# A wait in every third indirect transfer of a four-layer kernel, and a new order table

## The chip, the cores and the metric

The program runs on 1 core of one Trainium2 chip. The metric is device time in microseconds, from launch to the end of the program. The time of a kernel is the median over its runs; for the kernel before, six runs gave 665.21 to 668.11 us, median 667.08. Beside the timed runs there is one profiled execution, whose trace the views below come from.

The core has five engines that each run their own list of instructions in order: PE (matmuls; its weight loads are listed as PEld), DVE and ACT (vector and scalar work), POOL (slower vector work, and here all indirect transfers) and SP (it only issues transfers). They meet through semaphores. 16 DMA engines move the data.

## The reference, cut to what matters

The input is `x` of shape 8 x 512 x 128, that is 4096 tokens of 128 features. Four layers follow each other, each added to its input:

```python
x = x + L0_attn(layernorm(x))   # gated linear recurrence over 512 steps, 128 channels
x = x + L0_ffn(layernorm(x))    # one 128x128 linear, chosen among 8 by logits and noise
x = x + L1_attn(layernorm(x))   # delta rule: 16 heads, an 8x8 state each, 512 steps
x = x + L1_ffn(layernorm(x))    # mixture of experts
```

The last layer is the one that the change is about. For each token it picks two of eight experts:

```python
probs = softmax(xf @ w_router)
topk_w, topk_idx = top_k(probs, 2)
h = gelu(einsum('te,ieh->tih', xf, w1) + b1)      # 128 -> 512
out = einsum('tih,ihe->tie', h, w2) + b2          # 512 -> 128
out = sum(out * weights[..., None], axis=1)       # two experts have a weight
```

and the third layer fixes the pace of much of the kernel, since its state goes from step to step:

```python
retrieval = einsum('bhij,bhj->bhi', S, k_t)
S = S + einsum('bhi,bhj->bhij', beta_t * (v_t - retrieval), k_t)
o_t = einsum('bhij,bhj->bhi', S, q_t)
```

## The kernel before

**Tiles and groups.** A tile is 16 time steps of all 8 sequences, 128 rows. There are 32 tiles, taken in nine groups of 2, 4, 4, 4, 4, 4, 4, 4 and 2 (`SIZES`). Each group goes through the first two layers, then through the delta rule, whose steps are taken four at a time: 4 blocks a tile, 128 blocks in all, each a fixed row of DVE instructions (`prod`, `st`, `so`). The groups overlap: while DVE works on the blocks of one, ACT, PE and POOL prepare the next ones (`f`, `knq`, `dots`, `tmat`) and finish the earlier ones (`so`, `qkp`).

**The experts.** After the delta rule `route` finds each token's two experts. Groups are put together to sets (`GROUPS`: 2; 4+4; 4+4; 4+4; 4 tiles), five sets in all; the last group of 2 tiles is computed with every expert instead. For a set, `experts` computes on DVE a place for each row, sorted by expert and padded to whole blocks of 128 rows (`dest`, shown as `small_dest`). Then:

1. `scatter` sends each tile's rows to their places in a table in DRAM: one indirect transfer of 128 rows of 512 bytes for each tile and each of the two choices, issued by POOL (`places<-xne,small_dest`). That makes 4, 16, 16, 16 and 8 transfers, 60 in all.
2. `load_rows` reads four blocks of the sorted rows back (`xb<-places`, issued by SP). It waits for all scatters of the set.
3. PE transposes them (`ph<-ident,xb`), ACT copies the result (`xbT`), and for each block SP loads the weights of its expert (`w1b`), PE multiplies (`ph<-xbT,w1b`), ACT applies the gelu (`hid`), PE multiplies again (`po<-w_sb,hid`, or `in<-w_sb,hid` where another bank is used), and SP writes the outcome to a second table (`results<-yb`).
4. 60 indirect transfers fetch each token's two rows (`back<-results,small_dest`, POOL). They are weighted on ACT and summed on POOL (`fin`), for the last set both on DVE, and go out through DRAM (`out_rows`, `out`).

Two more indirect transfers fetch the weights of the second layer (`wsel`, `bsel`), so there are 122.

**The order.** No engine's order follows from the order of the source. All operations are first recorded in a `Plan` (`Recorder.record`, hence one line, L330, for most instructions) with their dependencies. A planner (`place`, `backward`) can put them in an order by costs and due times; there an indirect transfer starts no earlier than `WINDOW` microseconds after the one `BURST` places before it (`rows[-BURST] + WINDOW`), 6.0 us and 4 places. When the table `ORDER` has as many entries as there are operations, the planner is not used: `emit` goes through the 4796 numbers of `ORDER`, and `BANKS` gives the PSUM bank of each tile that has a choice. Each engine then executes its own operations in that order. POOL's operations are each tied to the one before; between scatters of one set some of these ties are dropped together with the dependency between their rows, so that scatters of one set can change places among themselves.

An indirect transfer occupies POOL while it is issued, and lands later. Its landing is told by one of eight semaphores, taken in turn, so a transfer waits, before and after the change, for the one eight before it.

**Names used below.** A "set" is one of the five groups of rows that go through the experts together. "The fourth set" has the 16 scatters between 473.5 and 503.5 us, "the fifth set" the 8 scatters between 545.6 and 556.8 us.

Of the kernel before, what the change touches and what calls it, by code (L numbers as in the profile page):

```python
# [69 lines left out]
class Plan:  # L70
# [4 lines left out]
    def __init__(self, tc, banks):  # L75
        self.tc, self.hw, self.banks = tc, tc.nc, banks
        self.ops, self.seen, self.key, self.slack = [], {}, 0.0, 0.0
        self.tensor, self.vector, self.scalar, self.gpsimd, self.sync = (
            Recorder(self, e) for e in ("tensor", "vector", "scalar", "gpsimd", "sync")
        )  # L80
# [213 lines left out]
    def emit(self):  # L294
        kind = mybir.EngineType
        with self.tc.manual_schedule(engines={kind.PE, kind.DVE, kind.Activation, kind.SP}):
            for op, switch in self.best():
                if switch:
                    self.hw.scalar.preload_act_table_set(switch)  # L299
                made = op.emit()  # L300
                if op.engine == "gpsimd":
                    self.tc.keep_in_program_order(made)

# [50 lines left out]
def _cost(engine, name, n, kw):  # L354
# [19 lines left out]
BURST, WINDOW = 4, 6.0  # L374
# [9 lines left out]
    3, 10, 38, 43, 36, 37, 45, 35, 34, 48, 44, 1, 5, 53, 0, 9, 50, 49, 57, 46, 7, 335, 52, 8, 11, 32, 51, 47, 33, 4,  # L384
    12, 59, 126, 39, 61, 58, 31, 2, 13, 6, 16, 14, 327, 67, 62, 15, 40, 129, 63, 17, 64, 54, 130, 65, 18, 131, 336,
    66, 19, 343, 132, 21, 323, 133, 435, 55, 134, 324, 830, 135, 68, 153, 70, 145, 154, 328, 69, 146, 106, 444, 160,
    101, 107, 100, 325, 77, 152, 42, 147, 163, 60, 108, 326, 102, 155, 161, 390, 103, 391, 104, 392, 337, 148, 393,
    109, 344, 338, 156, 110, 112, 71, 149, 394, 87, 111, 41, 150, 98, 136, 157, 113, 151, 339, 367, 399, 158, 114,
    162, 340, 418, 137, 351, 159, 72, 165, 164, 400, 329, 375, 167, 341, 401, 330, 56, 397, 359, 405, 115, 74, 166,
    128, 395, 331, 116, 168, 406, 117, 22, 342, 332, 118, 176, 105, 170, 407, 119, 398, 169, 29, 171, 182, 175, 185,  # L390
    120, 333, 172, 138, 183, 173, 73, 174, 184, 334, 396, 187, 408, 402, 423, 188, 177, 409, 191, 139, 178, 403, 80,
    197, 179, 180, 181, 140, 99, 186, 141, 205, 346, 142, 192, 189, 410, 193, 404, 190, 345, 198, 199, 411, 194, 81,
    195, 200, 196, 204, 347, 206, 207, 201, 202, 209, 422, 203, 143, 412, 208, 210, 211, 348, 413, 213, 212, 214,
    219, 414, 446, 220, 215, 221, 226, 445, 222, 216, 349, 90, 415, 23, 223, 217, 224, 416, 218, 225, 417, 227, 447,
    229, 420, 228, 91, 231, 448, 419, 449, 424, 450, 230, 232, 144, 233, 421, 425, 236, 451, 235, 360, 237, 452, 241,
    427, 383, 238, 453, 249, 239, 234, 352, 240, 121, 243, 368, 250, 428, 458, 27, 20, 350, 253, 242, 460, 244, 254,
    429, 248, 258, 257, 245, 246, 251, 459, 247, 259, 263, 252, 271, 464, 260, 255, 261, 262, 272, 465, 256, 275,
    265, 454, 466, 276, 280, 281, 264, 455, 307, 426, 266, 282, 122, 279, 283, 270, 267, 284, 273, 268, 285, 269,
    293, 481, 274, 309, 277, 294, 297, 278, 286, 287, 298, 288, 301, 456, 292, 467, 289, 290, 291, 295, 362, 302,
    457, 361, 303, 468, 296, 461, 299, 88, 354, 300, 462, 353, 304, 384, 89, 469, 305, 25, 363, 313, 306, 355, 312,  # L400
    92, 376, 315, 463, 316, 24, 317, 318, 319, 320, 93, 470, 321, 364, 356, 430, 84, 322, 641, 431, 127, 432, 78,
    433, 28, 85, 434, 314, 365, 436, 30, 477, 437, 311, 471, 310, 308, 438, 79, 439, 440, 385, 94, 472, 123, 473, 95,
    124, 644, 82, 96, 125, 643, 645, 474, 441, 83, 442, 642, 475, 443, 499, 86, 482, 357, 358, 515, 517, 487, 516,
    518, 476, 519, 369, 522, 386, 521, 479, 523, 1065, 524, 478, 483, 520, 646, 525, 647, 484, 648, 649, 480, 783,
    650, 740, 377, 526, 378, 485, 527, 370, 486, 528, 379, 371, 655, 677, 488, 657, 489, 372, 490, 380, 373, 491,
    492, 656, 494, 651, 493, 387, 661, 388, 389, 653, 495, 662, 496, 652, 663, 366, 497, 664, 529, 97, 654, 26, 665,
    509, 659, 498, 658, 530, 666, 531, 660, 532, 500, 667, 501, 533, 502, 504, 534, 505, 503, 506, 535, 507, 1066,
    536, 508, 668, 381, 537, 548, 374, 547, 510, 538, 545, 511, 1068, 512, 546, 549, 669, 539, 513, 550, 540, 514,
    543, 695, 551, 541, 711, 552, 575, 1069, 576, 573, 670, 544, 578, 577, 554, 712, 574, 542, 714, 579, 553, 580,
    555, 558, 678, 671, 586, 581, 560, 382, 559, 557, 562, 672, 561, 563, 556, 582, 564, 673, 565, 592, 566, 583,  # L410
    567, 675, 568, 584, 569, 593, 585, 715, 594, 713, 595, 588, 674, 679, 596, 716, 590, 717, 597, 676, 589, 718,
    754, 680, 599, 587, 600, 719, 755, 682, 598, 720, 605, 601, 721, 681, 722, 591, 723, 602, 683, 724, 606, 725,
    603, 570, 614, 726, 1067, 684, 604, 571, 727, 685, 572, 728, 686, 729, 1070, 687, 619, 613, 730, 1071, 1413, 688,
    1072, 731, 1073, 607, 689, 617, 1074, 732, 690, 611, 733, 608, 734, 753, 735, 618, 691, 609, 615, 736, 692, 738,
    737, 610, 620, 739, 625, 757, 1136, 741, 616, 693, 758, 621, 694, 759, 696, 760, 622, 626, 697, 761, 612, 742,
    627, 699, 743, 1137, 762, 1079, 698, 629, 1135, 756, 623, 763, 624, 744, 628, 764, 1081, 745, 765, 1075, 766,
    1080, 630, 767, 1085, 746, 768, 1077, 631, 1086, 769, 1076, 1087, 747, 770, 771, 748, 772, 749, 632, 773, 1088,
    774, 700, 633, 701, 1078, 775, 702, 634, 703, 750, 1089, 776, 705, 777, 635, 778, 779, 636, 780, 781, 637, 1416,
    1138, 1090, 784, 1178, 1082, 751, 1139, 785, 752, 1140, 786, 1179, 1141, 1415, 1083, 787, 704, 1142, 1177, 1164,
    788, 1414, 1143, 706, 1417, 789, 707, 1084, 1144, 790, 708, 1145, 709, 1146, 1418, 1091, 1147, 791, 710, 1419,  # L420
    1148, 1102, 1149, 1150, 1420, 782, 999, 1092, 1151, 1000, 1152, 1119, 792, 1153, 1093, 793, 1154, 794, 1155,
    1421, 1094, 795, 1002, 1422, 1206, 1156, 1157, 638, 1101, 796, 1158, 797, 1001, 1159, 1095, 1160, 1162, 1003,
    1161, 1096, 1004, 1005, 1097, 1010, 1180, 1165, 1220, 1166, 1181, 1099, 1221, 639, 1182, 1167, 1014, 1183, 1168,
    1007, 1184, 1219, 1098, 1169, 640, 1006, 1185, 1008, 1016, 1103, 1170, 1009, 1163, 1017, 1171, 1186, 1018, 1019,
    1187, 1172, 1100, 1104, 1020, 1173, 1174, 1012, 1021, 1013, 1188, 1105, 1189, 1106, 1107, 1190, 1022, 1191, 1023,
    1175, 2111, 1192, 1176, 1024, 1193, 1194, 1195, 1108, 1025, 1196, 1197, 1026, 1029, 1198, 1027, 1109, 1199, 1030,
    1028, 1200, 1110, 1201, 1111, 1031, 1202, 1112, 1043, 1037, 1203, 1204, 1427, 1032, 1222, 1262, 1113, 1205, 1038,
    1035, 1223, 1429, 1224, 1114, 1041, 1033, 1225, 1248, 1207, 1226, 1115, 1261, 798, 1428, 1208, 1040, 1227, 1209,
    1034, 1039, 1042, 1228, 1210, 1011, 1211, 1116, 1229, 1433, 1015, 1230, 1044, 1036, 1231, 799, 1232, 1263, 1434,
    1212, 1117, 1233, 1046, 1264, 1045, 1435, 1234, 1049, 1425, 1235, 1047, 1050, 1236, 1048, 1237, 1213, 1423, 1426,  # L430
    1238, 1052, 1239, 1214, 1051, 1240, 1215, 1053, 1241, 1216, 1424, 1242, 1217, 1243, 75, 1129, 1118, 1244, 1054,
    1246, 1218, 1436, 1245, 1247, 1304, 1437, 1249, 1482, 1265, 1250, 1055, 1266, 1251, 1267, 1431, 1268, 1252, 1253,
    1269, 1120, 1481, 1123, 1254, 1270, 1430, 1121, 1255, 76, 1483, 1271, 1256, 1122, 1124, 800, 1257, 1272, 1056,
    1273, 1438, 802, 1274, 1125, 1258, 1432, 1126, 1275, 1259, 1127, 1276, 1260, 1439, 801, 1595, 1277, 1128, 803,
    1278, 2112, 1130, 1279, 804, 1291, 1280, 1131, 1281, 1132, 1057, 1440, 1133, 1282, 824, 1058, 1283, 1134, 1466,
# [203 lines left out]
def seq_kernel(  # L639
# [70 lines left out]
    nc = Plan(tc, shared)  # L710
# [904 lines left out]
    def experts(group):  # L1615
# [67 lines left out]
        def scatter(at, src):  # L1683
            def emit():
# [6 lines left out]
                for before_ in scattered:  # L1691
                    tc.declare_no_dep(rows_out.ins, before_, reason="every row has places of its own")
# [107 lines left out]
        for g, _, weights in group["chunks"]:  # L1800
            n = SIZES[g]
# [219 lines left out]
```

## Time and profile before

| what | value |
|---|---|
| median of six runs | 667.08 us (665.21 to 668.11) |
| the profiled execution's own time | 661.0 us |
| its span (first to last instruction of the program) | 659.3 us |
| granted PE clock, mean | 0.92 |
| POOL, `places` transfers | 60, 59.8 us, 997 ns each |
| POOL, `back` transfers | 60, 58.5 us, 975 ns each |
| ACT, table loads | 64, 82.1 us, 1283 ns each |
| DVE, block recurrence (`so`, `st`, `prod`), per block | 684 + 497 + 491 + 426 + 284 + 291 ns |
| PE, `ph<-xbT,w1b` | 760, 141.1 us |
| HBM traffic over the span | 172 GB/s |

A group's line in the profile reads: source line, engine, operation, what is written and read, count, busy time, mean of one, and then the idle time of that engine just before these instructions with what ended it. In the slices, the span is cut into 40 parts of 16.5 us and a digit is the busy share in tenths. The chain of waits is followed back from the last instruction: at each step to whatever released it, or to the instruction before it on the same engine; its lines are start, length, and what. The waits of an engine read: who waited, for whom, microseconds in total, how many times, and the longest. In the lines of a timeline the bracket at the end is the engine's idle time before the instruction and what ended it; "issue" there means that the profile shows nothing that it waited for.

### The profile page before, as it was taken

The numbers are of one execution on the slowest core, as the hardware profiler recorded it, in microseconds if no ns is written. First come the engines' busy times: TensorE is split into PE (matmuls) and PEld (weight loads), VectorE is DVE, ScalarE is ACT, GpSimd is POOL, SyncE is SP. The second block draws the span as 40 slices with busy tenths as digits, with TensorE's granted clock in tenths as the row PEclk, the third lists the DMA queues.
The fourth block names the chain that finished last, engine by engine and source line by source line (L and its number), as shares of the span: only waits on it lengthen the run. The fifth ranks groups of instructions, "written<-read, shape, count | busy, mean of one in ns | idle before, by whom it ended". The sixth has DMA issues, their size and how long they took to land.

```text
span 659.3 us, 10937 instructions
## 1 busy us (share of the span) xinstructions
PE 523.3 (79%) x3077; PEld 408.4 (62%) x3077; DVE 464.1 (70%) x1290; ACT 468.2 (71%) x984; POOL 458.0 (69%) x603
## 2 busy tenths in 40 slices
PE   3885668677686688787988787999968988778886
PEld 3653333454544465674676575787958888777775
DVE  7666248999999999989799998999982770002021
ACT  2875797878878579988899997967855554536421
POOL 6545467769678748899996878886589687553340
PEclk9898678989789689979899797999999899998989
DMA  4948235335342657445776576798986877776641
GB/s 128 317 137 264 71 89 147 92 81 131 94 128 72 173 127 200 124 138 163 203 198 168 134 192 181 199 238 230 235 224 198 236 216 220 207 224 181 165 119 40
DMA packets 96721, 110.16 MB, mean 167 GB/s; under 512 B 10179, under 2 KB 68206, under 8 KB 96662
## 3 DMA queue, kind: packets, MB, share of 16 engines
q1 hardware_dynamic: 91984, 101.31, 55.7%
q0 software_dynamic: 3904, 8.00, 4.4%
q8 instruction: 26, 0.43, 0.3%
q14 instruction: 33, 0.27, 0.1%
q10 hardware_dynamic: 774, 0.15, 0.1%
HBM read 85.90 MB, written 27.48 MB: 172 GB/s over the span
## 4 chain that ended last, share of the span: by engine, by line
DVE 34%; PE 24%; ACT 14%; POOL 11%; issue 5%; DMA 2%; another core or an unknown queue 2%; DVEq 0%; POOLq 0%; ACTq 0%; SPq 0%
DVE st L330 17%; PE ph L330 9%; PE in L330 7%; DVE so L330 7%; POOL places L1685 5%; PE po L1747 3%; ACT L299 3%; DVE prod L330 3%; ACT f L330 3%; PE po L330 2%; ACT hid L330 2%; PE in L1747 2%; ACT b L330 2%; POOL so L330 2%
## 5 line engine op out<-in xcount | busy, mean ns | idle before, releaser
L330 PE MATMUL ph<-xbT,w1b 128*128 128x128 f32 x760 | 141.1, 287 | 13.3 <-ACT hid L330 6.0
L330 PEld LDWEIGHTS ph<-xbT,w1b 128*128 128x128 f32 x760 | 114.0, 200 | 20.8 <-ACT hid L330 8.3
L330 ACT ACTIVATE hid<-ph 128x512 f32<-128x512 f32 x111 | 65.5, 597 | 75.8 <-PE ph L330 44.3
L1747 PE MATMUL po<-w_sb,hid 128*128 x536 | 104.2, 285 | 3.4 <-ACT hid L330 2.8
L330 DVE TENSOR_TENSOR so<-kq,st 128x512 f32<-128x512 f32 x128 | 87.6, 684 | 7.4 <-DMA kq<-scratch 1.3
L1747 PEld LDWEIGHTS po<-w_sb,hid 128*128 128x128 f32 x536 | 83.6, 197 | 13.8 <-issue 8.5
L299 ACT ACT_TABLE_LOAD x64 | 82.1, 1283 | 8.8 <-DMA x<-in_L_attn_u_dram 7.7
L1685 POOL DMA_INDIRECT places<-xne,small_dest x60 | 59.8, 997 | 19.7 <-issue 10.8
L330 POOL DMA_INDIRECT back<-results,small_dest x60 | 58.5, 975 | 21.2 <-issue 13.7
L330 DVE TENSOR_REDUCE st<-st 128x64 f32<-128x320 f32 x128 | 63.6, 497 | 3.7
L330 DVE TENSOR_REDUCE st<-so 128x32 f32<-128x320 f32 x128 | 62.8, 491 | 3.9 <-ACT so L330 0.8
L330 DVE TENSOR_TENSOR st<-kq,st 128x256 f32<-128x256 f32 x128 | 54.5, 426 | 3.5
L330 PE MATMUL po<-wo,so 128*128 128x128 f32 x240 | 47.0, 297 | 12.0 <-POOL so L330 7.7
L330 PEld LDWEIGHTS po<-wo,so 128*128 128x128 f32 x240 | 39.1, 207 | 26.4 <-POOL so L330 10.5
L330 PE MATMUL in<-f,wT 128*128 128x512 f32 (+1 forms) x72 | 40.1, 651 | 7.8 <-DVE small_best L330 3.7
L330 PE MATMUL in<-b,wqkvb 128*128 128x512 f32 (+1 forms) x72 | 39.4, 635 | 8.5 <-DVE x L330 3.1
L1747 PE MATMUL in<-w_sb,hid 128*128 x224 | 45.1, 285 | 1.1 <-DVE small_where L330 1.0
L330 DVE TENSOR_TENSOR prod<-tmat,st 128x128 f32<-128x128 f32 x128 | 36.4, 284 | 7.0 <-POOL tmat L330 3.8
L330 POOL TENSOR_TENSOR f<-f,f 128x512 f32<-128x512 f32 (+1 forms) x27 | 32.4, 1200 | 12.3 <-ACT f L330 11.9
L330 DVE TENSOR_REDUCE st<-prod 128x32 f32<-128x128 f32 x128 | 37.3, 291 | 4.7
L330 POOL TENSOR_TENSOR so<-so 128x512 f32<-128x512 f32 x24 | 31.3, 1305 | 11.1 <-DVE so L330 8.2
L330 PE MATMUL ph<-ident,xb 128*128 128x128 f32 x95 | 28.1, 302 | 12.5 <-ACT hid L330 7.4
(339 smaller groups left out, 1366.7 us busy)
## 6 DMA issues: line engine op xcount, KB each, us to landing
kq<-scratch SPq DMA_DIRECT2D x64, 512.0 KB
w1b<-w1b_dram SPq DMA_DIRECT2D x103, 256.0 KB
xb<-places SPq DMA_DIRECT2D x20, 256.0 KB
results<-yb SPq DMA_DIRECT2D x20, 256.0 KB
places<-yb SPq DMA_DIRECT2D x2, 1472.0 KB
kq<-in_L_ffn_w_dram SPq DMA_DIRECT2D x2, 1024.0 KB
w1b_dram<-kq SPq DMA_DIRECT2D x2, 1024.0 KB
u_rows<-in_L_attn_u_dram SPq DMA_DIRECT2D x7, 256.0 KB
```

Source lines behind the costliest of these rows:

```text
L299: self.hw.scalar.preload_act_table_set(switch)
L330: return method(*(on(x) for x in args), **{k: on(x) for k, x in kw.items()})
L1685: rows_out = hw.gpsimd.indirect_dma_start(out=table[0 : nblk * P, :], out_offset=bass.IndirectOffsetOnAxis(ap=at, axis=0), in_=src, in_off ...
L1747: return hw.tensor.matmul(out_.on(nc.banks), lhsT=src, rhs=w2_f[:, bass.ds(at + c * P, P)], start=(c == 0), stop=(c == NHB - 1),)
```

## The change

The plan keeps a list `sent` of the indirect transfers that have been emitted, in the order of the table. When a transfer is emitted whose number in that list (from 0) is 3, 6, 9 and so on, it gets a dependency with a semaphore on the landing of the transfer emitted just before it. `scatter`, which otherwise declares that scatters of one set don't depend on each other, leaves this one dependency alone. `BURST` goes from 4 to 3 and `WINDOW` from 6.0 to 5.7; these two are read only by the planner and, `BURST`, by the new rule. `ORDER` and `BANKS` are replaced as a whole by tables that were made with these values; they hold the same operations in another order. No operation is added or taken away.

```diff
         self.ops, self.seen, self.key, self.slack = [], {}, 0.0, 0.0
+        self.sent = []
...
                 if op.engine == "gpsimd":
                     self.tc.keep_in_program_order(made)
+                if op.by_rows:
+                    landed = self.to_land()
+                    if landed:
+                        wait = mybir.DependencyInfo(mybir.DependencyClass.Sync, mybir.DependencyReason.DATA)
+                        self.tc.add_manual_dep(made.ins, landed, wait, reason="few indirect transfers at a time")
+                    self.sent.append(made.ins.name)
+
+    def to_land(self):
+
+        n = len(self.sent)
+        return self.sent[-1] if n and n % BURST == 0 else None
...
-BURST, WINDOW = 4, 6.0
+BURST, WINDOW = 3, 5.7
...
 ORDER = (
-    3, 10, 38, 43, 36, 37, 45, 35, 34, 48, 44, 1, 5, 53, 0, 9, 50, 49, 57, 46, 7, 335, 52, 8, 11, 32, 51, 47, 33, 4,
...
                 for before_ in scattered:
-                    tc.declare_no_dep(rows_out.ins, before_, reason="every row has places of its own")
+                    if before_ != nc.to_land():
+                        tc.declare_no_dep(rows_out.ins, before_, reason="every row has places of its own")
```

## The prediction

> **What bounds the kernel now.** The engine rows of the page come first: no engine is full over the whole span, so a sum over the kernel is worth little.
>
> ```profile
> PE 523.3 (79%) x3077; PEld 408.4 (62%) x3077; DVE 464.1 (70%) x1290; ACT 468.2 (71%) x984; POOL 458.0 (69%) x603
> DVE  7666248999999999989799998999982770002021
> POOL 6545467769678748899996878886589687553340
> ...
> q0 software_dynamic: 3904, 8.00, 4.4%
> ```
>
> DVE is at 9 in most slices from about 115 to 490 us: there the recurrence of the third layer (128 blocks) sets the pace. From about 490 us DVE empties and PE takes over. The windows show this from 425 us on, with PE against DVE and POOL.
>
> ```profile
> 425.00:470.00 45.00, 42.57 (x324) 37.58 (x324) 42.31 (x131) 32.03 (x69) 32.58 (x52) 1.00 0.90 238
> 470.00:512.00 42.00, 32.76 (x257) 30.10 (x256) 26.82 (x68) 27.01 (x57) 35.70 (x40) 1.00 0.79 213
> 512.00:565.00 53.00, 47.61 (x382) 45.44 (x383) 24.92 (x78) 26.84 (x58) 39.52 (x49) 0.97 0.76 221
> 565.00:655.00 90.00, 73.63 (x521) 66.96 (x519) 13.03 (x43) 38.80 (x80) 34.49 (x35) 0.96 0.55 160
> ```
>
> After each window's bounds and length stand the busy times of PE, PEld, DVE, ACT, POOL. In 470 to 512 us PE loses 9.2 of 42 us and POOL, at 35.7, is the fullest. What ties them is in the chain of waits in that window:
>
> ```profile
> 484.49 0.20 DVE x L330
> 484.69 1.00 POOL places L1685
> ...
> 501.77 0.98 POOL places L1685
> ...
> 503.47 4.14 DMA places<-xne,small_dest
> 507.69 4.41 DMA xb<-places
> 512.15 0.33 PE ph L330
> ```
>
> DVE hands the chain to POOL at 484.7 us. POOL works through the scatters of the fourth set of rows (16 `places` transfers, 473.5 to 503.5 us); the last must land before SP may load `xb`, and only then do PE's expert matmuls of that set begin, at 512.15. So a microsecond on POOL between those scatters is a microsecond on the path. The PE waits of 425 to 515 us give this one 1.8 us:
>
> ```profile
> PE ph L330 <- DMA xb<-places: 1.8, 1, 1.8
> ```
>
> PE already waits there, so it has no slack to give.
>
> **What a wait costs.** An indirect transfer holds POOL about 1 us and lands later. Five lines of POOL's timeline, from two stretches:
>
> ```profile
> 449.81 0.94 POOL L330 DMA_INDIRECT back<-results,small_dest  x1 [0.30 <-issue]
> 451.06 0.94 POOL L330 DMA_INDIRECT back<-results,small_dest  x1 [0.30 <-issue]
> ...
> 499.76 1.01 POOL L1685 DMA_INDIRECT places<-xne,small_dest  x1 [0.17 <-issue]
> 500.80 0.80 POOL L330 TENSOR_TENSOR so<-so,qkp 128x256 f32<-128x256 f32 x1
> 501.77 0.98 POOL L1685 DMA_INDIRECT places<-xne,small_dest  x1 [0.17 <-issue]
> ```
>
> Two adjacent transfers start 1.25 to 1.3 us apart (1.0 busy, 0.30 idle); with a tensor operation between, the idle time before the transfer is 0.17. The landing I take from the packets of queue 0: 3904 packets are 32 for each of 122 transfers, 16 of 4096 bytes and 16 of 4 bytes. Taken in order of issue, the sixteenth 4-byte packet of a transfer ends 1.87 us after its start at the earliest, 3.15 at the median, 4.28 at the 90th percentile. (The transfer of 503.47 is at 3.59 by this; the chain's 4.14 is when SP saw it.) I take 3.15 and, as an estimate, 0.1 for POOL to see the semaphore: 3.25. A waiting transfer directly behind the one it waits for then loses 3.25 - 1.30 = 1.95 us; with about 2 us of POOL work between, 1.27; with over 3.3, nothing.
>
> The Trainium skill, "DMA: Bandwidth & Descriptors", section "Anatomy of one DMA — SWDGE (gpsimd) path", fits 2.0 us plus the bytes by 436e3 per us. For 64 KB that is 2.15 us, an estimate from the page, against 3.15 measured here in a kernel whose DMA engines are 79% busy in 470 to 512 us. By the page a wait behind an adjacent transfer would cost about 0.85 us and the fourth set's last scatter would start at about 510 instead of the 514.5 worked out below. Its "most of it is waiting for the write receipt" speaks against this change: it makes POOL sit through a time that transfers in flight would share.
>
> **The change part by part.** It removes no instruction and adds no arithmetic. The built program has the same matmuls, DMAs and vector operations on each engine, 62 table loads instead of 64 (2 x 1.28 us on ACT, mean 1283 ns in the groups), and 40 waits, at transfers 3, 6, ... 120 of the table's order. Where nothing else stands between the pair (15 of the 40) the loss is 1.95; summed over all forty with the POOL work that really stands between each pair, POOL loses about 36 us (11 if a wait ends 1.97 after the start, 67 at 4.4: the ends 1.87 and 4.28 with the same 0.1). POOL is idle 201 of 659 us, so the question is where.
>
> First three sets (219 to 425 us). Waits cost 1.95 + 0.8 + 1.4 us, and the gathers around 450 another 2.2. In the windows from 113 to 470 us POOL is idle 72 of 357 us and DVE sets the pace; nothing behind these waits (`so`, `qkp`, `tmat`) is late by more than that idle time covers. I take 0; if the cover were gone it would be the 6.3 us.
>
> Fourth set. Counting only POOL, by rows: before, 15 transfers x 1.0 + 13 tensor operations 12.1 + gaps 3.2 = 30.3 us from first scatter to last (measured 29.9; the method holds). After, the new table puts 18 tensor operations between the same scatters: 15.0 + 16.4 + 2.9 = 34.3. The five more are a `so`, a `fin`, two `dots`, a `tmat`, 4.3 us that were done later before. Five waits lie in it, with 4.70, 1.30, 1.98, 1.30, 1.98 us between start and wait: 0 + 1.95 + 1.27 + 1.95 + 1.27 = 6.4. So 40.8 us, +10.5 by the same count. Its first scatter follows a DVE instruction (`small_dest`) that stands at place 1082 of DVE's order instead of 1083, so I start it at the same 473.5. Queued behind on POOL are the last tile group's `tmat` (DVE waits 3.75 us for it at 514.4 now; later by about 6.5) and, behind the landing, SP's `xb` load and PE. PE's new order holds 8 more matmuls ahead of that set's first transpose, 8 x 0.285 = 2.3 us of cover. Net: +8.2 us at PE. With a wait that ends at 1.97 (last scatter +5.4) it is +3; with 4.38 (+15.0), +12.7.
>
> Fifth set. Its last scatter by the same running count is at 567.0, against 551.1 by count and 556.8 measured before. Then 3.15 to land and 4.4 for `xb` give 575; PE reached those transposes at 568.2 before and would now at about 576. The two meet: I take 0 more. With 4.38 the scatter is at 578.3 and PE idles some 10 us; with 1.97 nothing.
>
> Gathers (505 to 640 us): 24 of the 36 us of waits, but POOL already idles there, as its waits show:
>
> ```profile
> POOL fin L330 <- ACT back L330: 29.8, 5, 9.7
> POOL back L330 <- DMA results<-yb: 5.2, 2, 4.1
> ```
>
> The last eight gathers run 628.2 to 637.9 and lose 4 us; their sums end on DVE at 642.4 and two copies out follow, the last issued at 644.95, while PE works until 653.2. That cover is about 8 us. I take 0.
>
> The table loads: 2.6 us of ACT, which is busy 71%; 0 on this path, at most 2.6 won.
>
> Sum: 0 + 8.2 + 0 + 0 = +8.2 us on an execution of 661.0 us (span 659.3). The runs shown have a median of 667.08, 6 us above that execution; the difference is put on the median: **675 us**.
>
> **The rivals.**
> *The fifth set decides too.* If landings are nearer 4.38 than 3.25 because DMA is busy (0.90 of it in 425 to 470), the fourth set gives +12.7 and the fifth some 8 to 10 more: about 688. For it: the transfers of 447 to 463 us took 4.1 to 5.9 to land. Against: at the fifth set the present ones took 1.9 to 3.9.
> *The new table is faster than its waits are slow.* In 113 to 470 us DVE is idle 25.2 us (357 less 331.8). An order that saves half of it, with the two table loads, brings the fourth set 12.6 + 2.6 us forward and loses 8.2: -7, 660 us. It decides from the point where the set's first scatter comes 8.2 us before 473.5. Against: DVE's instructions ahead of that scatter are the same in number, and the single waits in those windows are under 2 us.
> *The waits do next to nothing.* If landings at the waits are 1.9, and the fifth set's row numbers, which DVE now casts after block 123 instead of 128, help PE: +3 less 2 or 3, 667.
>
> **How the numbers follow.** Forecast (about +8): 0.50. Fifth set too: 0.24. Faster table: 0.18. Nothing: 0.08. The measurement tells no change within 0.3%, 2 us. Faster 0.18, same 0.08, slower 0.74. Range: from the low bound less part of the order's gain, 661, to the upper rival's 690; the forecast's own range is 670 to 681.
>
> **What would show it.** Right: POOL gaps of about 2 us before every second or third transfer; the fourth set's scatters taking about 40 us instead of 30; PE idle some 9 to 10 us for `xb` at one place near 515 to 525; nearly unchanged PE and DVE busy sums. Wrong: scatters of the fourth set starting well before 473 us, DVE through its 112th block earlier, or the chain not passing POOL there at all. A long PE wait near 570 would be the first rival. A larger share of the tail on POOL's gathers would say that the cover of 8 us was misjudged.

## The result and the profile after

| | median | runs | range |
|---|---|---|---|
| before | 667.70 us | 46 | 659.55 to 673.51 |
| after | 676.54 us | 20 | 671.31 to 682.83 |

The ratio after to before is 1.0141, 95% interval 1.0119 to 1.0164: slower by 1.4%, about 9 us. The profiled execution of after took 681.4 us (span 679.5), 4.9 us over its own median, while that of before (661.0) lay 6.7 us under its own. The two spans differ by 20.2 us, so differences between these two profiles overstate the change, and the experiments below carry the sizes.

The page of after: the engines' rows, and POOL's row of slices.

```profile
PE 525.4 (77%) x3077; PEld 415.2 (61%) x3077; DVE 461.2 (68%) x1290; ACT 466.5 (69%) x982; POOL 457.7 (67%) x603
POOL 6454568769777859887986986876668477534441
```

The same work is spread over 20 us more. PE's busy sum is 2 us larger and that of its weight loads 7 us, the others are up to 3 us smaller. What grew most is waiting. The windows that were shown of before, now of after (the same columns):

```profile
425.00:470.00 45.00, 38.30 (x286) 33.62 (x287) 41.24 (x116) 31.54 (x67) 35.52 (x48) 1.00 0.84 229
470.00:512.00 42.00, 33.71 (x227) 30.18 (x225) 31.80 (x92) 26.71 (x54) 25.93 (x35) 0.92 0.75 209
512.00:565.00 53.00, 43.00 (x307) 41.34 (x308) 23.48 (x80) 24.71 (x48) 37.41 (x49) 0.87 0.60 175
565.00:655.00 90.00, 77.57 (x573) 71.86 (x572) 6.25 (x27) 43.20 (x93) 43.96 (x44) 0.94 0.66 193
```

From 470 to 512 us POOL's busy time fell from 35.7 to 25.9 us: it stands at waits, 4.3 us of them for DVE ahead of the fourth set's first scatter, which starts at 478.5 us instead of 473.5. From 512 to 565 us PE does 307 matmuls where it did 382. The chain of waits of this profile can be followed only over the last 24 of 680 us, so the fourth set is read from POOL's timeline:

```profile
485.11 1.01 POOL L1697 DMA_INDIRECT places<-xne,small_dest  x1 [0.17 <-issue]
487.65 0.96 POOL L1697 DMA_INDIRECT places<-xne,small_dest  x1 [1.53 <-DMA places<-xne,small_dest]
...
501.59 1.01 POOL L1697 DMA_INDIRECT places<-xne,small_dest  x1 [0.17 <-issue]
507.36 0.96 POOL L1697 DMA_INDIRECT places<-xne,small_dest  x1 [4.76 <-DMA places<-xne,small_dest]
...
511.51 1.27 POOL L342 TENSOR_TENSOR so<-so 128x512 f32<-128x512 f32 x1
```

The bracket at the end is the new wait: the second scatter of each pair starts when the first has landed, 2.54 and 5.77 us after the first began. Behind the wait of 507.36 stand a `so` at 511.51 and, behind the next scatter, its second part at 513.98 to 514.78; PE needs that tile and goes on at 514.83. PE's waits from 500 to 540 us:

```profile
PE in L342 <- POOL so L342: 5.7, 1, 5.7
PE in L342 <- POOL small_taken L342: 2.6, 1, 2.6
```

And POOL's waits over the whole run that a landing ended (who waited, for what, total, times, longest):

```profile
POOL back L342 <- DMA back<-results,small_dest: 31.2, 10, 4.5
POOL places L1697 <- DMA places<-xne,small_dest: 15.2, 7, 4.8
POOL places L1697 <- DMA back<-results,small_dest: 1.7, 1, 1.7
```

That is 48 us, two thirds of it in front of gathers. Before, POOL had no wait that the landing of an indirect transfer ended. Three more waits of the changed kernel belong here, though the view puts them to "issue": the transfers 99, 108 and 117 start 4.7, 1.4 and 5.1 us after POOL became idle, and 1.2 to 1.5 us after the last packet of the transfer ahead of them. With them it is 59 us. The rows "issue" of before and after, and transfer 99:

```profile
POOL back L330 <- issue: 13.7, 48, 0.6
POOL back L342 <- issue: 21.5, 43, 5.1
608.65 0.95 POOL L342 DMA_INDIRECT back<-results,small_dest  x1 [4.70 <-issue]
```

### The profile page after: what moved, and what is told of

Read it like the earlier page. It is cut to its first block, busy times and chain, and to the rows that moved or that the text cites. A ratio compares the mean times of both kernels' runs of the same rounds, so it can differ in the third digit from the quotient of the medians.

```text
span 679.5 us, 10948 instructions
## 1 busy us (share of the span) xinstructions
PE 525.4 (77%) x3077; PEld 415.2 (61%) x3077; DVE 461.2 (68%) x1290; ACT 466.5 (69%) x982; POOL 457.7 (67%) x603
## 5 line engine op out<-in xcount | busy, mean ns | idle before, releaser
L1760 PE MATMUL po<-w_sb,hid 128*128 x672 | 132.4, 293 | 8.1 <-ACT hid L342 5.2
L342 PEld LDWEIGHTS ph<-xbT,w1b 128*128 128x128 f32 x760 | 115.0, 203 | 32.2 <-ACT hid L342 20.2
L1760 PEld LDWEIGHTS po<-w_sb,hid 128*128 128x128 f32 x672 | 108.2, 206 | 18.5 <-issue 10.6
L342 PE MATMUL po<-wo,so 128*128 128x128 f32 x208 | 40.3, 307 | 21.5 <-POOL so L342 15.7
L342 PEld LDWEIGHTS po<-wo,so 128*128 128x128 f32 x208 | 34.2, 214 | 31.5 <-POOL so L342 22.6
L342 PE MATMUL in<-b,wqkvb 128*128 128x512 f32 (+1 forms) x72 | 37.4, 605 | 6.0 <-ACT f L342 2.2
L342 PE MATMUL in<-f,wT 128*128 128x512 f32 (+1 forms) x72 | 38.2, 619 | 4.1 <-ACT qkp L342 1.2
L342 POOL TENSOR_TENSOR f<-f,f 128x512 f32<-128x512 f32 (+1 forms) x27 | 31.0, 1150 | 13.7 <-ACT f L342 11.5
L342 PE MATMUL in<-wo,so 128*128 128x128 f32 x112 | 24.1, 320 | 9.8 <-POOL so L342 7.7
L342 ACT ACTIVATE back<-back,small_weight 128x128 f32<-128x128 f32 x52 | 19.2, 395 | 16.6 <-DMA back<-results,small_dest 16.6
```

Source lines behind the costliest of these rows:

```text
L342: return method(*(on(x) for x in args), **{k: on(x) for k, x in kw.items()})
L1760: return hw.tensor.matmul(out_.on(nc.banks), lhsT=src, rhs=w2_f[:, bass.ds(at + c * P, P)], start=(c == 0), stop=(c == NHB - 1),)
```

## The experiments

Three sets of four kernels ran, each set on one chip together with runs of before; ratios are to those runs. Before took 647.9, 647.9 and 647.3 us there, 20 us less than in the runs of the result, and the changed kernel 673.1. The ratios are those of the record; the quotient of the two medians differs from them by up to 0.004, 2.7 us. Unless a diff says otherwise, a kernel is the changed one with one line altered, so table and banks are the new ones. PE, DVE and ACT run the same order in all kernels with the new table. POOL's order is not wholly fixed by the table: with the waits up to four of its 603 instructions stand elsewhere than without, and none in the kernel with 98 to 113 only. The transfers are numbered as in the prediction; the fourth set's scatters are 50 to 65, the gathers and the fifth set's scatters 66 to 121.

| kernel | waits at | median us | ratio to before | 95% |
|---|---|---|---|---|
| before once more | none | 647.35 | 1.0014 | 0.9985 to 1.0042 |
| changed kernel once more | all 40 | 673.12 | 1.0408 | 1.0371 to 1.0445 |
| new table alone | none | 648.42 | 1.0003 | 0.9969 to 1.0038 |
| without the fourth set's | 35 | 666.41 | 1.0319 | 1.0271 to 1.0367 |
| without the last eight gathers' | 37 | 671.51 | 1.0366 | 1.0333 to 1.0399 |
| fourth set only | 5 | 654.92 | 1.0095 | 1.0059 to 1.0131 |
| ahead of the fourth set only | 16 | 652.23 | 1.0067 | 1.0043 to 1.0091 |
| behind the fourth set only | 19 | 665.30 | 1.0272 | 1.0239 to 1.0306 |
| 66 to 97 only | 11 | 652.80 | 1.0051 | 1.0016 to 1.0086 |
| 98 to 113 only | 5 | 656.14 | 1.0115 | 1.0068 to 1.0161 |
| all 40, for the third ahead | 40 | 649.53 | 1.0004 | 0.9969 to 1.0039 |
| old table with the waits | 40 | 697.60 | 1.0736 | 1.0682 to 1.0790 |

**The changed kernel and the kernel before, once more.** No edit.

> The changed kernel once more, for a second profile and as the yardstick of this batch. Its first profiled execution took 681.4 us, 5 us over its median of 676.5, so a difference of single microseconds can't be read from that trace alone. All theories: 676.5, ratio to the kernel before 1.014. In the trace: fourth set of scatters about 41 us from first to last (41.7 in the first trace, 29.9 before).

> The kernel before, unchanged, for a profile beside the runs that follow. In the first four runs it took 648 us on their chip against 667 on the chip of the result, while the changed kernel took 673 and 676. Theory 1 (the order without waits is as early here as the new table without waits was): casts of the fourth set near 470, its last scatter near 500 to 505, last scatter of the fifth set near 555, last accumulation near 638, time equal to the baseline within 0.3%. Theory 2 (before gains from something else than the cast of set four): cast near 473 as in the first profile and the 20 us come after 515, in the tail alone.

The changed kernel takes what it took in the result within 0.5%, but before is 20 us faster, so the change costs 26 us here (0.0408 of 648). Between the two profiles of before the casts of the fourth set (473.1 and 473.9 us) and the last scatters of the fifth (556.8 and 556.0) agree; the last accumulation is at 653.8 in the first and 638.1 in the second. Theory 2 holds for what the profiles show: they differ by 15.7 us, and 14.9 of these lie between the fifth set's last scatter and the last accumulation. ACT's waits from 560 to 640 us, first profile of before ("remote" is an event that the profile ties to no instruction):

```profile
ACT hid L330 <- remote: 10.5, 3, 3.8
ACT xbT L330 <- remote: 3.3, 1, 3.3
```

The second profile has no such wait there, only waits for PE and for gathers. So the kernel before lost some 15 us between 565 and 640 us in the first profile, 13.8 of them at four places where ACT waits for something that the profile doesn't tell and PE, as far as it waits there, mostly waits for ACT. The profile of after has such waits too; from 490 us to its end:

```profile
ACT hid L342 <- issue: 8.9, 5, 2.6
ACT xbT L342 <- remote: 1.3, 1, 1.3
ACT xbT L342 <- issue: 0.9, 1, 0.9
```

These are 11.1 us; in the first profile of before the waits of ACT under "remote" and "issue" over the same stretch are 22.6 us, and in the twelve profiles of the experiments there are none, but for 1.9 us in the old table with the waits. So these pauses belong to the runs of the result, in both kernels. Whether to their chip or to something else wasn't settled.

**The new table without waits.**

```diff
-        return self.sent[-1] if n and n % BURST == 0 else None
+        return self.sent[-1] if n and n % BURST == 0 and False else None
```

> The new tables with none of the 40 waits. Theory W (the waits cost, the table little): the fourth set falls from about 41 to 34 us (15 transfers, 18 tensor operations and gaps), POOL's idle time that ends with a landing falls from 48 us to nearly 0, and the time to about 669 (the five tensor operations moved in front, 4.3 us, less 2.3 of PE cover, stay). Rival T (the new table is what costs, the waits fall into idle time): 675 to 677. Rival G (the new table alone is a gain that the waits eat): under 665.

1.0003: the new order by itself neither costs nor gains. All of the loss needs the waits.

**The old table with the waits.** `ORDER` and `BANKS` are those of before, the rest is the change.

```diff
 ORDER = (
-    19, 38, 42, 327, 31, 71, 35, 57, 18, 1, 9, 0, 45, 422, 418, 60, 335, 14, 11, 343, 15, 351, 74, 58, 13, 106, 48,
...
+    3, 10, 38, 43, 36, 37, 45, 35, 34, 48, 44, 1, 5, 53, 0, 9, 50, 49, 57, 46, 7, 335, 52, 8, 11, 32, 51, 47, 33, 4,
...
```

> The table of before with the forty waits at transfers 3, 6, ... 120 of its own order. If the time goes to the waits and the table matters little, ratio 1.035 to 1.045, as for the changed kernel (1.041). If the new table, made under the rule, hides part of them, this is slower than the changed kernel by over 3 us (ratio over 1.046); if the new table is the worse of the two, under 1.035.

1.0736, which is 48 us over before (0.0736 of 648) where the new table loses 26. So the second outcome holds, by far: the table made under the rule takes away nearly half of what the waits cost. The forty waits stand before other transfers here, and about 14 of POOL's 603 instructions stand elsewhere than in before, so this prices the two tables under the rule and not the waits one by one. POOL's waits for landings in this kernel are longer and more:

```profile
POOL back L342 <- DMA back<-results,small_dest: 43.1, 14, 7.0
POOL places L1697 <- DMA places<-xne,small_dest: 17.0, 7, 5.1
```

**The waits part by part.** The line of `to_land` ends in turn with these conditions:

```diff
-        return self.sent[-1] if n and n % BURST == 0 else None
+        return self.sent[-1] if n and n % BURST == 0 and 50 <= n < 66 else None
```

> New table, waits only at the five places in the fourth set's scatters. The prediction's theory (these five waits are what the change costs): 6.4 us over the table without waits, ratio to before near 1.010. Rival (the waits are covered singly and only cost together): under 3 us, ratio under 1.005.

1.0095, or 6.0 us over the table alone: the prediction's 6.4 for the five waits holds. The set takes 41.0 us from first scatter to last, against 35.0 without waits. Their removal from the changed kernel (`and not 50 <= n < 66`) says the same, 6.7 us between the medians and 5.8 by the ratios. The waits are five, at 51, 54, 57, 60 and 63, where the expectation says six; 35 stay.

> The changed kernel without the six waits at transfers 51 to 63, those of the fourth set; the other 34 stay. If the fourth set decides, as the prediction has it, it gives back about 6.4 us: 670, with the set at about 34 us and PE's first transposes of that set some 6 us earlier. Rival (fifth set and tail set the end anyway): 675 to 676. Rival (many small delays before the set): 673 to 675, and the set starts as late as in the changed kernel.

```diff
+        return self.sent[-1] if n and n % BURST == 0 and n < 50 else None
```

> New table, only the sixteen waits ahead of the fourth set. The prediction took them as covered by idle time of POOL: ratio 1.000 to 1.003, the cast of row numbers for the fourth set near 470 as without waits. Rival (they delay the recurrence): the cast near 475, 5 to 6 us, ratio near 1.009.

The ratio is nearer the rival's: 0.0064 over the table alone, 4 us. But the rival's mark, the cast of the fourth set's rows near 475, does not decide: it is at 477.3 here and between 469.7 and 477.0 in five profiles without these waits. The second set's scatters take 40.2 us, first to last, instead of 36.8. Where the 4 us are lost is not resolved by one profile.

```diff
+        return self.sent[-1] if n and n % BURST == 0 and n >= 66 else None
```

> New table, only the nineteen waits behind the fourth set (gathers and the fifth set's eight scatters). The prediction took them as covered, with 4 us at most at the end: ratio 1.000 to 1.006. Rival (fifth set and gathers are on the path): 9 to 13 us, ratio 1.014 to 1.020, groups of eight gathers at 14 to 18 us instead of 9, last accumulation near 650.

1.0272, some 17 us: the largest part by far, one that the prediction set to zero, and more than the rival's 9 to 13. The three parts, 0.0092, 0.0064 and 0.0269, add up to 0.0425 against 0.0405 for all waits, so within their intervals they act one by one. To see which of the nineteen count, they were split:

```diff
+        return self.sent[-1] if n and n % BURST == 0 and 66 <= n < 98 else None
```

> New table, waits only among transfers 66 to 97 (gathers mixed with the fifth set's scatters; eleven waits). Theory A (the waits behind the fourth set cost in two places: the fifth set's scatters come later, and gathers that land late hold ACT and with it PE): about 9 to 10 us here, ratio 1.013 to 1.016, last scatter of the fifth set 8 us later than without waits, PE idle longer for xb. Rival B (only the gathers of 98 to 121 cost): under 3 us, ratio under 1.005.

1.0051, 3 us over the table alone (5 by the medians): at the bound of rival B, and below theory A. The fifth set's last scatter does come later (50.0 us after the last `tmat`, 44.7 without waits), but from there to the last accumulation it is 78.1 us instead of 81.2, so 3 us of it are won back. PE's waits hold none for `xb`; the longest is this:

```profile
PE in L342 <- POOL small_taken L342: 4.8, 1, 4.8
```

```diff
+        return self.sent[-1] if n and n % BURST == 0 and 98 <= n < 114 else None
```

> New table, waits only among transfers 98 to 113 (gathers of the fourth set; five waits). Theory A: ACT reaches a scaling of a gathered row that is not there yet, the exponent-side activation of the next expert tile stands behind it in ACT's order, PE idles 5 us once and then runs at half its clock for some 4 us: 6 to 8 us, ratio 1.009 to 1.012. Rival B' (these gathers have slack, ACT's wait is covered): under 2 us, ratio under 1.003, no PE idle of over 3 us behind ACT hid.

1.0115, 7 us from five waits: theory A, in size and in place. A line of POOL's timeline of this kernel, and then ACT's:

```profile
598.85 0.94 POOL L342 DMA_INDIRECT back<-results,small_dest  x1 [3.75 <-DMA back<-results,small_dest]
...
597.48 0.22 ACT L342 ACTIVATE small_prob<-small_prob 128x16 f32<-128x16 f32 x1
602.34 0.69 ACT L342 ACTIVATE back<-back,small_weight 128x128 f32<-128x128 f32 x2 [4.65 <-DMA back<-results,small_dest]
603.05 1.28 ACT L300 ACT_TABLE_LOAD   x1
604.34 1.09 ACT L342 ACTIVATE hid<-ph 128x512 f32<-128x512 f32 x2
```

and PE's beside it:

```profile
599.33 0.39 PE L1760 MATMUL in<-w_sb,hid 128*128 x2
604.99 1.65 PE L342 MATMUL ph<-xbT,w1b 128*128 128x128 f32 x6 [5.27 <-ACT hid L342]
606.43 0.64 PE L1760 MATMUL po<-w_sb,hid 128*128 x2
```

ACT stands 4.65 us before scaling a gathered row, that of the transfer of 598.85, which POOL, itself waiting, has issued late. Behind it in ACT's order are a table load and the `hid` of the next expert tiles, whose matmuls were done before 599.7. PE has nothing left and idles 5.27 us; then a pair of matmuls takes 0.64 us instead of 0.39. The wait of PE for ACT's `hid` from 500 us to the end, first without waits, then with these five:

```profile
PE ph L342 <- ACT hid L342: 0.8, 2, 0.5
```

```profile
PE ph L342 <- ACT hid L342: 6.7, 3, 5.3
```

In the profile of after the same place is there, with the same three instructions on ACT:

```profile
620.26 0.69 ACT L342 ACTIVATE back<-back,small_weight 128x128 f32<-128x128 f32 x2 [5.39 <-DMA back<-results,small_dest]
620.98 1.28 ACT L300 ACT_TABLE_LOAD   x1
622.27 1.08 ACT L342 ACTIVATE hid<-ph 128x512 f32<-128x512 f32 x2
```

Last, the changed kernel without the waits of the last eight gathers (`and n < 114`):

> The changed kernel without the waits at transfers 114, 117 and 120, those of the last eight gathers. The prediction took them as covered by about 8 us: no change, 676.5. The trace of the changed kernel speaks against that: DVE takes the last sums in order between the every-expert sums, and PE waits 3.4 us for one of these (acc) behind a late gather. If that is the path: 673.

1.0366 against 1.0408: 2 to 3 us by medians and by ratios, but an interval that overlaps that of the changed kernel. The gathers themselves go from 14.0 to 8.8 us. The pieces of the nineteen (3, 7 and at most 3) make 13 of the 17 us; the remaining 4 are no more than the intervals of these runs, 2 to 3 us to either side, leave open.

**The same forty waits, for an earlier transfer.**

```diff
-        return self.sent[-1] if n and n % BURST == 0 else None
+        return self.sent[-3] if n and n % BURST == 0 else None
```

> New table, the same forty waits, each for the transfer issued three ahead instead of one ahead. If the cost is the landing that remains after the issue (3.05 us median from the start, 1.25 to 1.3 us between adjacent starts), three starts are 3.8 us or more and little remains: POOL's idle ended by landings falls from 45 us to under 8, ratio 1.000 to 1.006. If a wait costs by itself (the semaphore, the queue's order), it stays near 1.03.

1.0004 (by the medians 2 us more than before, inside the interval). A wait costs by what remains until the landing, not by itself: three starts back, that is little. POOL's waits for landings were expected under 8 us and are about 14, and the time doesn't show it:

```profile
POOL back L342 <- DMA back<-results,small_dest: 7.2, 7, 3.0
POOL places L1697 <- DMA places<-xne,small_dest: 5.0, 2, 4.4
```

No kernel tried is faster than before; this one and the new table alone equal it within their intervals.

## Why the prediction was right in sum, and where it was wrong

The sum said +8.2 us and the result is +8.8. By parts, it was right in the waits of the fourth set and wrong in the rest, and it met the total because of a thing that it couldn't see.

*What a wait costs: right on average in the fourth set, too low over the run.* 3.25 us from start to start were taken. The four waits that bind in the fourth set took 2.54, 2.81, 5.77 and 2.53 us in the profile of after, mean 3.41: three below the price and one far above, so the mean is partly luck. The 0.1 us for POOL to see the landing is shown by no run: at 17 of the 18 such waits in the profile of after POOL starts 0.6 to 1.5 us (median 0.7) after the last packet of the transfer ahead. Landings, counted as before from the packets of queue 0, have a median of 3.05 us (3.15 before), 1.86 at the least and 4.55 at the 90th percentile. POOL's waits for landings are 48 us over the run, 59 with the three under "issue", where 36 were summed. The fit of the Trainium skill, "DMA: Bandwidth & Descriptors", section "Anatomy of one DMA — SWDGE (gpsimd) path", gave 2.15 us for such a transfer, an estimate; the measurement has it between the least and the median, so the trace's price was the better one here. (The words about the write receipt that the prediction puts in quotation marks are a paraphrase: the page's table gives "~most of the 2 µs" for it.)

*Fourth set: right in its waits, wrong in the rest.* The scatters take 41.7 us first to last (40.9 in the second run), as forecast: 40.8. The waits' 6.4 are 6.0 and 6.7 by two experiments. (From 473.5 the 40.8 us lead to 514.3; the 514.5 in the prediction is a slip.) But the first scatter starts at 478.5 (476.0 in the second run) and not at 473.5, so the last is at 520.2; profiles of the new table without the waits ahead have it anywhere from 470.2 to 477.5, so no run shows what moves it. The 4.3 us for five more tensor operations are in the set (35.0 us first to last without waits, against 34.3 by count) but not in the time: the table alone costs nothing, so what is done earlier is not missed later. The place was wrong as well. PE was to idle 9 to 10 us for `xb`; it idles 5.7 us for a `so` that POOL reaches only after the waits. I had named `tmat` and `xb` as queued behind the scatters, and left out `so`.

*First three sets: wrong.* "I take 0" measured 4 us. The bound that was given, 6.3, holds it.

*Fifth set: half wrong.* Its last scatter was to be at 567.0 and is at 578.3, with the fourth set already starting 5 us later than taken; the waits from 66 to 97 cost 3 us, with no long wait of PE near 570. That rival's total (688) was not reached, and its mechanism not found.

*Gathers: the step that failed.* "24 of the 36 us of waits, but POOL already idles there ... I take 0." I asked only whether POOL had time, and followed what stands behind a gather for the last eight alone. The waits among 98 to 113 cost 7 us because the gathered row is scaled on ACT, in order, ahead of the `hid` that PE needs; POOL's idle time is no cover for that. The last eight may add 2 to 3, where no loss at all was forecast; the intervals overlap.

*Why the sum held.* In the experiments the change costs 26 us, three times the forecast. In the result it costs 9, because before was 20 us slower there while after took nearly the same time as here. From the last scatter of the fifth set to the last accumulation the profiles read:

| profile | us |
|---|---|
| before, of the result | 97.0 |
| after, of the result | 95.7 |
| before once more | 82.1 |
| new table alone | 81.2 |
| changed kernel once more | 90.0 |

In the runs of the result, the stretch where the gathers' waits cost 8 to 9 us was already as long before as after. The four unexplained pauses of the kernel before are in it, and part of those of after. Why they cost before 15.7 us between the two profiles, but after 9.4 (and 20 against 3 by the medians), stays open; that the waits are hidden there because the pauses come first is argued from these profiles, not shown. So the number was right by luck: terms set to zero that are worth some 20 us, and a baseline slow in the same place.

*The rival "the new table is faster than its waits are slow"* fell: without waits it gains nothing. But the table was no bystander, since with the waits it is 21 us better than the old one (0.0736 less 0.0408). The prediction had not weighed that at all.

## What to carry to other kernels

Idle time of the engine that waits is no cover by itself: follow what it issues to the engine that uses it, and ask what stands behind that use in that engine's order. If the number of transfers in flight must be bounded, wait for one issued several places ahead rather than the last, where the looser bound will do: here the same forty waits cost 26 us or nothing that the runs can tell. And take a second profile of the kernel before where a forecast rests on its tail, because the 20 us between two sets of runs of one program were here more than twice the change that was forecast.

## What the runs showed of the hardware

- The same program took 667.7 us in the runs of the result and 647 to 648 on each of the three chips of the experiments, with 13.8 us of it in four waits of ACT that the profile ties to nothing. The changed kernel differed by 3.4 us. Such waits stand in both profiles of the runs of the result and, but for 1.9 us, in none of the twelve others.
- A waiting indirect transfer starts 0.6 to 1.5 us after the last packet of the one that it waits for (17 of the 18 such waits in the profile of after), so the wait is longer than the packets show.
- After the idle time of 6 us before 622.9 us, PE's granted clock was half for some 4 us; so it was after the 5.27 us in the kernel with the waits 98 to 113 (0.50 from 604 to 608 us). The windows of after around it, where the clock is the third number from the end of a line (0.50, then 0.92):

```profile
622.00:626.00 4.00, 3.08 (x14) 3.08 (x15) 0.00 (x0) 2.52 (x7) 2.52 (x3) 0.50 0.06 16
626.00:630.00 4.00, 3.85 (x26) 3.16 (x25) 0.27 (x1) 2.14 (x5) 2.42 (x3) 0.92 0.54 149
```

  PE does 14 matmuls in the first four microseconds and 26 in the next: by half the clock over nearly 4 us, this stall cost about 2 us more than it lasted, an estimate. The Trainium skill, "TensorE: Matmul & The Clock Gate", section "Part 1: The HAM clock gate (the "warmup" mystery)", has the rule: after an idle window of some 3.4 us the clock falls to half until about as much time has been worked. The rows agree, with an idle time of 6.02 us ahead and half the clock until 626.
